# One gather tile in every eighth group of a graph-network kernel, fetched row by row from SyncE

## The chip, the cores and the metric

The kernel runs on one core of a Trainium2 chip. The metric is the device time of one launch, in microseconds, taken as the median of several runs.

The core has five engines that the text names: TensorE (PE for its matmuls, PEld for its weight loads), VectorE (DVE), ScalarE (ACT), GpSimd (POOL) and SyncE (SP), which computes nothing and issues DMAs. [...] A suffix q, as in SPq, is the engine's own sequencer, where DMA issues, register loads and waits stand.

## What is computed

One message-passing layer over a graph of 6250 nodes with 128 features and 100,000 edges that are sorted by destination. Cut to what matters:

```python
msg_in = concat([x[src], x[dst], edge_attr], axis=1)       # 100000 x 260
h = silu(msg_in @ mW1 + mb1)
messages = h @ mW2 + mb2
aggregated = segment_sum(messages, dst, num_segments=6250)
u = silu(concat([x, aggregated], axis=1) @ uW1 + ub1)
out = layernorm(x + layernorm(x + (u @ uW2 + ub2)))
```

Everything is float32. The first matrix is split by rows, so that the part of `x[src]` can be multiplied before the rows are gathered: a table `tab_a = x @ mW1[:128]` is made once in HBM, and an edge then needs one row of it, 512 bytes. This gather of 100,000 rows is what the change touches.

## The kernel before, in words

The edges are cut into groups of 1024, eight tiles of 128 edges each (`G = 8`, `GE = 1024`), which makes 98 groups, the last one shorter. One pass of the main loop (L688) handles one group. The order of instructions on every engine is the order in which the program writes them, as a manual schedule is in force for all five engines.

In pass g the following stand in this order:

- `load(g + 4)` (L593) on SP. It fetches `mv`, 96 rows of a second table `tab_b` that begin at a row number held in a register (L599), and `st`, the edge attributes (L600). Every fourth time it also fetches `near` (L320), the destination numbers of four groups at once, 384 KB; every 14th time `load_bases` (L344) loads 14 row numbers from SBUF into registers of SP and DVE. The `mv` buffers are five, so the fetch for group g + 4 has to wait until TensorE has done the products of group g - 1. In some passes other DMAs are issued by SP too: `xs` and `out_dram` of a node batch (L495, L572), and the turning of edge attributes (L306, L313).
- `hidden(g)` (L640): DVE adds the gathered rows `ga` and the products `pre` into `s` (L648), ACT makes `h` of it (L649).
- `products(g + 2)` (L627) on TensorE (L631), from `st` and `mv`.
- `node_matrix(g + 3)` (L602), which reads `near` (DVE, L604), and `edge_matrix(g + 1)` (DVE, L617).
- `by_nodes(g)` (L665), the segment sum of the group by matmuls (TensorE, L660), and its addition to the accumulator two passes later.
- `fetch(g + 2)` (L273): eight gathers on POOL, one for each tile (L277). Each reads 128 row numbers from SBUF[...] and starts their transfer into `rows[g + 2][:, i, :]`. The first of them waits for the first product of group g + 2, the fifth for the first sum of group g.
- a step of each node batch that is under way.

SP has eight semaphores for its DMAs and takes them in turn. Before it issues a DMA it therefore waits until the DMA eight places earlier has landed.

Of the kernel before, what the change touches and what calls it, by code (L numbers as in the profile page):

```python
# [8 lines left out]
F32 = mybir.dt.float32  # L9
I32 = mybir.dt.int32  # L10
# [4 lines left out]
ENG = mybir.EngineType  # L15
# [3 lines left out]
P = 128  # L19
EPS = 1e-5  # L20
IN_RANGE = "indices of nodes, which the reference takes to be in range"
# [3 lines left out]
def kernel(  # L25
# [40 lines left out]
    nc = tc.nc  # L66
    N, H = x.shape
# [4 lines left out]
    G = 8  # L72
    GE = G * P
    NG = -(-E // GE)
# [2 lines left out]
    NW = NP + W  # L77
    K1 = W + ED
    RB = 14
    CLOSE = 14  # L80
    LEAD = 4
    RAW = 5
# [7 lines left out]
    EJ = EC // EQ  # L90
    assert NG % RB == 0 and EC * NC == E and EJ * EQ == EC

# [16 lines left out]
    work = edges.enter_context(tc.tile_pool(name="edge", bufs=2))  # L109
# [154 lines left out]
    tab_a = dram.tile([NP, H], F32, name="tab_a")  # L264
# [2 lines left out]
    near_d = dram.tile([NG, GE], U8, name="near_d")  # L267
    rows, bases, near = {}, {}, {}

    def tiles_of(g):  # L270
        return min(G, -(-(E - g * GE) // P))

    def fetch(g, *after):  # L273

        rows[g] = gath.tile([P, G, H], F32, name="ga")
        for i in range(tiles_of(g)):
            ins = nc.gpsimd.indirect_dma_start(  # L277
                out=rows[g][:, i, :],
                out_offset=None,
                in_=x if g < RAW else tab_a[:, :],  # L280
                in_offset=bass.IndirectOffsetOnAxis(
                    ap=src_i[:, g, i : i + 1] if g else src_0[:, i : i + 1], axis=0
                ),
            )
            part, at = divmod(i * len(after), G)
            if after and at == 0 and after[part]:
                tc.add_manual_dep(
                    ins.ins,
                    after[part].ins.name,
                    mybir.DependencyInfo(  # L290
                        mybir.DependencyClass.Sync, mybir.DependencyReason.DATA
                    ),
                    reason="TensorE keeps up with the gathers",
                )

    fetch(0)


# [4 lines left out]
    def attributes(c):  # L303
        t = turn.tile([EQ, EJ * ED], F32, name="ea_l")
        chunk = edge_attr[c * EC : (c + 1) * EC]
        nc.sync.dma_start(t, chunk.rearrange("(q j) d -> q (j d)", q=EQ))  # L306
        ea_l[c] = t
# [7 lines left out]
    def destinations(g):  # L315

        n = min(NQ, NG - g)
        t = work.tile([W, NQ, GE], U8, name="near")
        flat = near_d[g : g + n].rearrange("(o g) e -> o (g e)", o=1)
        nc.sync.dma_start(  # L320
            t[:, :n].rearrange("w g e -> w (g e)"), flat.to_broadcast([W, n * GE])
        )
        for k in range(n):
            near[g + k] = t[:, k, :]
# [18 lines left out]
    def load_bases(g):  # L343
        _, vals = nc.values_load_multi_w_load_instructions(  # L344
            base_i[0:1, g : g + RB],
            engines=(ENG.SP, ENG.DVE),
            min_val=0,
            max_val=NP,
            skip_runtime_bounds_check_because=IN_RANGE,
        )  # L350
        for k, v in enumerate(vals):
            bases[g + k] = v
# [63 lines left out]
    ps = edges.enter_context(tc.tile_pool(name="edge_ps", bufs=2, space=PSUM))  # L416
# [5 lines left out]
    def node_y():  # L422
        return node_ps.tile([P, BT, H], F32, name="y")
# [13 lines left out]
    def load_weights():  # L437
        for name, shape in (("w2", [P, H]), ("u1a", [P, H]), ("mb2", [P, 1])):
            raw_w[name] = work.tile(shape, F32, name=f"raw_{name}", bufs=1)
        nc.sync.dma_start(raw_w["w2"], mW2)  # L440
        nc.sync.dma_start(raw_w["u1a"], uW1[P:])
        nc.sync.dma_start(raw_w["mb2"], mb2.rearrange("(f o) -> f o", o=1))
        nc.sync.dma_start(u1x, uW1[:P])
        nc.sync.dma_start(u2, uW2)
        nc.sync.dma_start(ub1_col, ub1.rearrange("(f o) -> f o", o=1))
        nc.sync.dma_start(ub2_row, ub2.rearrange("(o f) -> o f", o=1))
        for t, row in ((g_b, ln_g), (b_b, ln_b), (ub2_b, ub2)):
            nc.sync.dma_start(t, row.rearrange("(o f) -> o f", o=1).to_broadcast([P, H]))

    def fuse_weights():  # L450
        pm = node_y()
        nc.tensor.transpose(pm[:, 0, :], raw_w["w2"], ident)
        yield
        w2T = work.tile([P, P], F32, name="w2T", bufs=1)
        nc.scalar.copy(w2T, pm[:, 0, :])
        yield
        nc.tensor.matmul(pm[:, 1, :], w2T, raw_w["u1a"], start=True, stop=True)
        nc.tensor.matmul(pm[0:1, 2, :], raw_w["mb2"], raw_w["u1a"], start=True, stop=True)
        yield
        nc.scalar.copy(w2u, pm[:, 1, :])  # L460
        nc.vector.memset(mb2u, 0.0)
        for k in range(DQ):
            nc.scalar.copy(mb2u[32 * k : 32 * k + 1], pm[0:1, 2, :])
# [129 lines left out]
    def load(g):  # L593

        if g % NQ == 0 and g:
            destinations(g)
        if g % RB == 0 and g:
            load_bases(g)
        nc.sync.dma_start(mv[g % NM][:W], tab_b[bass.ds(bases[g], W), :])  # L599
        nc.sync.dma_start(stbuf[g % NST][W:], ea_d[:, g * GE : (g + 1) * GE])  # L600

    def node_matrix(g):  # L602

        nc.vector.tensor_scalar(  # L604
            stbuf[g % NST][:W],
            near.pop(g),
            p_next,
            0.0,
            op0=OP.is_equal,
            op1=OP.add,  # L610
            accum_out=deg_q[g // DQ % 2][:, g % DQ * 32 : g % DQ * 32 + 1],
        )
# [27 lines left out]
    def hidden(g):  # L640
        h = hbuf[g % NH]
        ga = rows.pop(g)
        n = tiles_of(g)
        s = pre.pop(g)
        if g >= RAW:
            ps = s
            s = work.tile([P, G, H], F32, name="s")
            nc.vector.tensor_add(s[:, :n], ga[:, :n], ps[:, :n])  # L648
        nc.scalar.activation(h[:, :n], s[:, :n], AF.Silu)  # L649
        return h  # L650

# [13 lines left out]
    def by_nodes(g, h, oh):  # L665

        pt = degrees(g)
        sums(g, pt, h, oh, 0, tiles_of(g))
        return pt
# [18 lines left out]
    for g in range(NG):  # L688
        if g == 1:
            load_weights()  # L690
        if g == 2:
            running.append(destination_checks(node_y()))
        if g == 8:
            running.append(fuse_weights())
        for c in range(1, NC):
            if g == max(1, c * EC // GE - 10):
                attributes(c)
            if g == max(1, c * EC // GE - 10) + 1:
                attribute_rows(c)
        if g + LEAD < NG:  # L700
            load(g + LEAD)
        last = g >= NG - 1
        if not last:
            h[g] = hidden(g)
        if g + 2 < NG:
            pre[g + 2] = products(g + 2)
        if g + MADE < NG:
            node_matrix(g + MADE)
        if g + 1 < NG:
            oh[g + 1] = edge_matrix(g + 1)  # L710
        if g - 2 in pt:
            add(g - 2, pt.pop(g - 2))
        if last:
            break
        pt[g] = by_nodes(g, h.pop(g), oh.pop(g))
        if CLOSE <= g + 2 < NG:
            fetch(g + 2, begun[g + 2], summing[g])
        elif g == 0:
            fetch(7, ended[1], begun[2])
        elif g == 1:  # L720
            fetch(8, begun[3], summing[1])
        elif g % 2:
            fetch(g // 2 + 8, ended[g + 1], begun[g + 2] if g == CLOSE - 3 else ended[g + 2])
        if g >= NG - 3:
            add(g - 1, pt.pop(g - 1))
        for i0, n, first in batches[:-1]:
            if g == (first if first >= NG - 3 else first + 1):
                running.append(node_batch(i0, n, *node_tiles(nodes, node_y)))
        for _ in range(0 if g == NG - 2 else 4 if g == NG - 3 else 2 if g >= NG - 6 else 1):
            advance(running)  # L730
        if g == NG - 3:
            final = node_batch(
                *batches[-1][:2],
                nodes,

                lambda name, p=P: gath.tile([P, G, H], F32, name="ga")[:p, :BT],
                lambda: rows_ps()[:, :BT],
                final=True,
            )
            next(final)  # L740
        if g == NG - 2:
            next(final)

    g = NG - 1
    n = tiles_of(g)
    ga, pg, oh_g, h_g = rows.pop(g), pre.pop(g), oh.pop(g), hbuf[g % NH]
    s = work.tile([P, G, H], F32, name="s")
# [27 lines left out]
    def all_nodes():  # L775
        with tc.tile_pool(name="nodes_g", bufs=2) as nodes:
            with tc.tile_pool(name="nodes_g_ps", bufs=1, space=PSUM) as node_ps:
                for i0, n, _ in batches:
                    y = lambda: node_ps.tile([P, BT, H], F32, name="y")
                    running = [node_batch(i0, n, *node_tiles(nodes, y))]  # L780
                    while running:
# [4 lines left out]
                         skip_runtime_bounds_check_because="the result of a comparison")  # L786
# [143 lines left out]
```

## Time and profile before

| | us |
|---|---|
| time before, median of 3 runs (1167.98 to 1169.18) | 1169.08 |
| time of the profiled execution | 1007.52 |
| its span, first to last instruction | 1005.4 |
| POOL busy | 740.0 (74%) |
| PE busy | 682.9 (68%) |
| DVE busy | 487.0 (48%) |
| ACT busy | 238.9 (24%) |
| mean granted TensorE clock | 0.739 |

The profiled execution is shorter than the timed runs by 161.56 us: the timed ones are 1.160 times as long. Durations below are those of the profiled execution. A group's line gives the summed busy time and the mean of one instruction, then the idle time of the engine ahead of it and what ended most of that. "Issue" is time in which the engine waited for nothing that the profile shows. Instructions of a sequencer, among them all DMA issues and register loads of SP, are not counted as busy.

### The profile page before, as it was taken

The page shows a single profiled execution, that of the slowest core. Times are in us where ns is not written, and L with a number is a line of the kernel's source. Part 1 is how long each engine was busy: PE and PEld are TensorE (multiplying, and loading weights), DVE is VectorE, ACT ScalarE, POOL GpSimd, SP SyncE. Part 2 cuts the span into 40 slices and gives each one's busy share as a digit, 9 for nine tenths or more (in the row PEclk, how much of TensorE's full clock was granted, in tenths as well). Part 3 has the DMA queues.
Part 4 walks back from the last instruction along what each step waited for, and adds up shares of the span by engine and source line. Part 5 has one row for each costly group of instructions (what it writes and reads, how often), then busy time and mean ns, then how long its engine had stood idle before and what let it go on. Part 6 is the DMA issues. An engine that isn't in the chain of part 4 may idle for free. (4 is left out here: it accounts for less than half of the span.)

```text
span 1005.4 us, 11309 instructions
## 1 busy us (share of the span) xinstructions
PE 682.9 (68%) x3645; PEld 627.6 (62%) x3645; DVE 487.0 (48%) x1018; ACT 238.9 (24%) x295; POOL 740.0 (74%) x790
## 2 busy tenths in 40 slices
PE   5869766577676567757676756767757666766854
PEld 4759756567666566756665755766656666565752
DVE  5667625444544543643554453544453454264455
ACT  2312212220321131231222122122023113122233
POOL 7767777777777777777777777777777777777771
PEclk9979977777767677667667667667767775867776
DMA  9954332232323322333233224232332332322221
GB/s 229 266 159 115 98 76 58 75 93 77 85 75 83 85 76 57 86 83 97 54 96 87 68 63 113 60 93 65 88 84 75 83 75 76 83 59 76 66 76 29
DMA packets 70076, 89.01 MB, mean 89 GB/s; under 512 B 20703, under 2 KB 51694, under 8 KB 70010
## 3 DMA queue, kind: packets, MB, share of 16 engines
q0 software_dynamic: 25024, 51.30, 20.7%
q1 hardware_dynamic: 40408, 35.03, 12.4%
q10 hardware_dynamic: 4578, 1.89, 0.9%
q8 instruction: 31, 0.51, 0.2%
q14 instruction: 35, 0.29, 0.1%
HBM read 76.78 MB, written 11.38 MB: 88 GB/s over the span
## 5 line engine op out<-in xcount | busy, mean ns | idle before, releaser
L277 POOL DMA_INDIRECT ga<-tab_a,src_i x742 | 700.7, 944 | 231.1 <-issue 210.0
L631 PE MATMUL pre<-mv,st 100*128 100x128 f32 x1564 | 328.6, 390 | 282.1 <-DVE s L648 235.6
L631 PEld LDWEIGHTS pre<-mv,st 100*128 100x128 f32 x1564 | 300.5, 293 | 304.4 <-DVE s L648 255.5
L648 DVE TENSOR_TENSOR s<-ga,pre 128x1024 f32<-128x1024 f32 x92 | 112.3, 1221 | 460.1 <-DMA ga<-tab_a,src_i 459.5
L660 PE MATMUL pt<-oh,h 128*128 128x96 f32 x1564 | 254.0, 332 | 7.2 <-DVE deg L678 3.9
L660 PEld LDWEIGHTS pt<-oh,h 128*128 128x128 f32 x1564 | 252.9, 253 | 9.4 <-ACT acc_b L500 3.3
L649 ACT ACTIVATE h<-s 128x1024 f32<-128x1024 f32 x92 | 97.2, 1057 | 649.1 <-DVE s L648 649.1
L604 DVE TENSOR_SCALAR_CACHE_REDUCE st<-near,p_next 96x1024 f32<-96x1024 uint8 x98 | 124.2, 1269 | 2.2 <-issue 1.4
L617 DVE TENSOR_TENSOR oh<-w_row,rel 128x768 f32<-128x768 f32 x98 | 93.0, 949 | 11.5 <-PE pt L660 11.5
L277 POOL DMA_INDIRECT ga<-in_x_dram,src_i x32 | 30.3, 948 | 9.8 <-issue 8.8
L649 ACT ACT_TABLE_LOAD x23 | 29.5, 1283 | 26.0 <-DMA raw_mb<-in_L_gnn_mb_dram 19.6
L489 ACT ACT_TABLE_LOAD x24 | 30.8, 1283 | 7.9 <-DVE mv L484 7.5
L530 PEld LDWEIGHTS y<-u,uT 128*128 128x128 f32 x94 | 22.5, 323 | 8.9 <-issue 8.9
L530 PE MATMUL y<-u,uT 128*128 128x128 f32 x94 | 25.2, 415 | 0.0
L678 DVE TENSOR_TENSOR deg<-deg,pt 1x96 f32 x98 | 24.4, 249 | 1.0
L673 DVE TENSOR_TENSOR acc<-acc,pt 128x96 f32 x98 | 23.6, 241 | 0.1
L377 PE MATMUL wide<-w,xT 128*128 128x256 f32 x98 | 23.1, 391 | 0.2 <-DVE rel L200 0.2
L377 PEld LDWEIGHTS wide<-w,xT 128*128 128x128 f32 x98 | 18.9, 198 | 2.9 <-DVE rel L200 0.4
L484 DVE BATCH_NORM_AGGREGATE mv<-st 128x2 f32<-128x6 f32 x98 | 17.8, 182 | 3.4
L568 ACT ACTIVATE z<-z,shift,r 128x128 f32<-128x128 f32 x47 | 19.2, 479 | 0.3 <-DVE shift L562 0.3
L545 DVE SCALAR_TENSOR_TENSOR z<-y,r,xs 128x128 f32<-128x128 f32 x47 | 16.5, 351 | 1.7
L542 DVE SCALAR_TENSOR_TENSOR y<-y,mv,g_b 128x128 f32<-128x128 f32 x47 | 16.5, 351 | 1.3
(118 smaller groups left out, 327.5 us busy)
## 6 DMA issues: line engine op xcount, KB each, us to landing
ga<-tab_a,src_i POOLq DMA_INDIRECT x742, 2.6
near<-near_d SPq DMA_DIRECT2D x24, 384.0 KB
mv<-tab_b SPq DMA_DIRECT2D x98, 48.0 KB
tab_a<-t SPq DMA_DIRECT2D x6, 512.0 KB
tab_b<-x_sb SPq DMA_DIRECT2D x6, 512.0 KB
xs<-in_x_dram SPq DMA_DIRECT2D x11, 256.0 KB
out_dram<-z SPq DMA_DIRECT2D x11, 256.0 KB
st<-ea_d SPq DMA_DIRECT2D x98, 16.0 KB
```

The costliest lines, as they stand in the source:

```text
L277: ins = nc.gpsimd.indirect_dma_start(out=rows[g][:, i, :], out_offset=None, in_=x if g < RAW else tab_a[:, :], in_offset=bass.IndirectOffs ...
L377: ins = nc.tensor.matmul(pm[:, j], xT[:, cols], w1, start=True, stop=True)
L489: nc.scalar.activation(r[:, :n], mv[:, :n, 1], AF.Sqrt, bias=eps)
L530: nc.tensor.matmul(y[:, i, :], by_p[:, :, i], u2, start=final, stop=final or i == n - 1)
L604: nc.vector.tensor_scalar(stbuf[g % NST][:W], near.pop(g), p_next, 0.0, op0=OP.is_equal, op1=OP.add, accum_out=deg_q[g // DQ % 2][:, g % D ...
L617: nc.vector.tensor_tensor(oh, w_row[:, None, :].to_broadcast([P, G, W]), rel[:, g, :, None].to_broadcast([P, G, W]), op=OP.is_equal,)
L631: ins = nc.tensor.matmul(pre[:, i, :], st[:, i, :], mv[g % NM], start=True, stop=g >= RAW)
L648: nc.vector.tensor_add(s[:, :n], ga[:, :n], ps[:, :n])
L649: nc.scalar.activation(h[:, :n], s[:, :n], AF.Silu)
L660: ins = nc.tensor.matmul(pt[:, :W], h[:, i, :], oh[:, i, :], start=i == 0, stop=i == tiles_of(g) - 1)
L673: nc.vector.tensor_add(at, at, pt[:, :W])
L678: nc.vector.tensor_add(at, at, pt[row, W:])
```

## The change

In nine groups, 24, 32, 40 and so on to 88, the eighth tile is no longer gathered by POOL. SP fetches it, one DMA of 512 bytes for each of its 128 rows, with the row number in a register. The work for such a tile is spread over eight passes: in each of the passes from `to - 10` to `to - 3`, after `load`, SP loads 16 row numbers into registers with one instruction and issues 16 DMAs. In the first of these passes it also fetches the 128 row numbers into SBUF. The tile has a buffer of its own, `ga_s`, so DVE adds it to the products in an instruction of its own, and the other addition is one tile shorter.

```diff
+    SPAN = 8
+    by_sync = {g: None for g in range(CLOSE + SPAN + 2, NG - SPAN + 1, SPAN)}
     def fetch(g, *after):
         rows[g] = gath.tile([P, G, H], F32, name="ga")
-        for i in range(tiles_of(g)):
+        for i in range(tiles_of(g) - (g in by_sync)):
             ins = nc.gpsimd.indirect_dma_start(
...
+    def fetch_by_sync(g):
+        for to in by_sync:
+            k = g - (to - SPAN - 2)
+            if not 0 <= k < SPAN:
+                continue
+            lo, hi = k * P // SPAN, (k + 1) * P // SPAN
+            if k == 0:
+                by_sync[to] = work.tile([P, H], F32, name="ga_s")
+                sources = work.tile([1, P], I32, name="src_s")
+                e0 = (to * G + G - 1) * P
+                nc.sync.dma_start(sources, src[e0 : e0 + P].rearrange("(o p) -> o p", o=1))
+                source_rows[to] = sources
+            _, vals = nc.values_load_multi_w_load_instructions(
+                source_rows[to][0:1, lo:hi],
+                engines=(ENG.SP,),
+                min_val=0,
+                max_val=N - 1,
+                skip_runtime_bounds_check_because=IN_RANGE,
+            )
+            for p, v in zip(range(lo, hi), vals):
+                nc.sync.dma_start(by_sync[to][p : p + 1, :], tab_a[bass.ds(v, 1), :])
...
     def hidden(g):
...
             s = work.tile([P, G, H], F32, name="s")
+            if g in by_sync:
+                n -= 1
+                nc.vector.tensor_add(s[:, n], by_sync[g], ps[:, n])
             nc.vector.tensor_add(s[:, :n], ga[:, :n], ps[:, :n])
+            n = tiles_of(g)
         nc.scalar.activation(h[:, :n], s[:, :n], AF.Silu)
...
         if g + LEAD < NG:
             load(g + LEAD)
+        fetch_by_sync(g)
```

In the built program SP has, for each row, a register operation that works out the address and the DMA; the row's DMA waits for nothing but its semaphore's turn. POOL's list is shorter by nine gathers and otherwise the same. DVE has nine additions of 128x128 more, each of which waits for all eight DMA semaphores of SP.

More of the change, by code (lines that the diff above doesn't have):

```diff
@@ L600, in load @@
         nc.sync.dma_start(stbuf[g % NST][W:], ea_d[:, g * GE : (g + 1) * GE])
+    def fetch_by_sync(g):
[19 more added lines that the diff above has]
+                nc.sync.dma_start(by_sync[to][p : p + 1, :], tab_a[bass.ds(v, 1), :])
+    source_rows = {}
     def node_matrix(g):
```

## The prediction, made before the changed kernel ran

> **What bounds the kernel now.** I began with the busy table and the costliest groups. No engine is over 74% busy, but POOL's gathers have idle time ahead of them that nothing ended:
>
> ```profile
> L277 POOL DMA_INDIRECT ga<-tab_a,src_i x742 | 700.7, 944 | 231.1 <-issue 210.0
> L648 DVE TENSOR_TENSOR s<-ga,pre 128x1024 f32<-128x1024 f32 x92 | 112.3, 1221 | 460.1 <-DMA ga<-tab_a,src_i 459.5
> ...
> SPq L599 <- PE pre L631: 274.9, 39, 10.8
> SPq L572 <- ACT z L568: 166.4, 11, 21.2
> SPq L313 <- ACT ea_t L311: 158.3, 9, 27.4
> SPq L495 <- DVE st L483: 129.4, 11, 32.8
> ```
>
> POOL's 0.94 us and the 0.30 us after it are one step. The timeline of POOL shows them back to back:
>
> ```profile
> 499.52 0.94 POOL L277 DMA_INDIRECT ga<-tab_a,src_i  x1 [0.31 <-issue]
> 500.77 0.94 POOL L277 DMA_INDIRECT ga<-tab_a,src_i  x1 [0.30 <-issue]
> 502.01 0.94 POOL L277 DMA_INDIRECT ga<-tab_a,src_i  x1 [0.30 <-issue]
> ```
>
> So a gather costs 1.249 us, 782 of them 977 us of the 1005.4, and eight make the pass of 9.99 us (s starts 159.9 us into the span in pass 14 and 879.3 in pass 86). DVE waits for gathers in nearly every pass. SP, last four lines of the first fence (time waited, times, longest), sleeps most of the time. What it does when it is awake matters here, so I read its own timeline and the durations of its instructions:
>
> ```profile
> 68.10 0.30 SPq L446 DMA_DIRECT2D ub_row<-in_L_gnn_ub_dram  x1
> ...
> 503.65 0.33 SPq L599 DMA_DIRECT2D mv<-tab_b  x1
> 504.02 0.33 SPq L600 DMA_DIRECT2D st<-ea_d  x1
> 504.58 0.33 SPq L599 DMA_DIRECT2D mv<-tab_b  x1
> ...
> L344 SPq TENSOR_LOAD <-base_i x7: 1356/3068/3358, 46.6 to 795.4; - x7
> ...
> L599 SPq FUSED_REGOPS  x98: 37/37/51, 58.9 to 933.5; - x98
> L599 SPq MOVE mv<-tab_b x98: 29/29/37, 59.1 to 933.6; - x98
> ```
>
> One `mv` and one `st` that wait for nothing take 504.58 - 503.65 = 0.93 us. A load of 14 registers takes 1.36 or about 3.1 us (minimum, median and maximum are shown).
>
> [...] Here the issue time is the whole matter, as the trace shows the DMA engines 0.31 busy from 150 to 880 us. [...] The trace agrees in the long loads (3068 / 14 = 219 ns) and not in the short ones (1356 / 14 = 97 ns). [...] the timed runs are 1.160 times the profiled one, in a kernel whose span is 97% gather steps. I take the gap between them for a scale, not for a constant, and multiply by 1.16.
>
> **Part by part.** *Removed:* nine gathers on POOL, 9 x 1.249 = 11.2 us, while POOL sets the pace. *DVE:* nine additions of 128x128, near 0.25 us each (the 128x96 addition at L673 means 241 ns), nine others shorter by an eighth (0.15 us), and some 0.3 us of semaphore waits: under 0.5 us in nine passes, hidden under DVE's waits for gathers (394 us from 150 to 880). Without that cover it is 4 us. *DMA traffic:* 1152 rows less on one queue, as many more on another: nothing.
>
> *SP, per pass, in passes 14 to 85:* the row's step is FUSED_REGOPS to MOVE 0.09, MOVE to DMA 0.06, the DMA, and 0.04 to the next. Single-row DMAs took 0.22 to 0.27 us (four lists at L131 and L133, 2.6 and 4 KB) and 0.30 us (`ub_row`, 512 bytes). I take 0.28, which makes 0.475; the ends are 0.42 and 0.52 (with the 0.33 of `mv`). Sixteen are 7.6 us. The register load of 16: at 97 ns 1.55 us, at 219 ns 3.5. Of the loads before, those whose first byte lies on a multiple of 16 were short, but for the first, which ran at 46.6 us, when the DMA engines were at 99%; the others were long. The new loads all begin on a multiple of 16, so I take 1.59 with the gap behind it. With `mv` and `st` 0.94, `near` every fourth pass 0.09, the node and attribute DMAs 0.17, the fetch of row numbers with its landing (0.37 + 2.2 in eight passes, as a load must wait for it) 0.32, the register load of L344 0.16 and occasional slow issues (1.64 and 1.68 us in the trace) 0.13, a pass costs SP **11.0 us**. Before, the same sum without the change was 1.5.
>
> That is more than the 9.99 us of POOL's pass. SP becomes the bound, but not at once. It runs ahead: in pass 20 it had issued its loads at 216.4, s began at 222.8, so the lead was 6.4 us (in undisturbed passes about 24, but the waits at L495, L572 and L313 bring it back to the engines every eight to ten passes). And it can fall behind a little, because loads are for later groups. The tightest is `near`: pass 4m - 4 of SP issues what DVE needs in pass 4m - 3, landing after some 4.6 us; with the addition after it, s of pass 4m - 2 starts 8 us after SP's pass began, two passes (22.6 us) earlier in number, so the engines may be 14.6 us ahead of SP. `mv` is needed in pass g + 2 and the rows in pass `to`, three passes after the last are issued: looser. From pass 20 to 86, 66 passes: 66 x (11.0 - 9.99) = 67 us late, less 6.4 and 14.6, leaves 46 us. Behind the late `near` stands DVE's own queue (L604, then L617 and the next s), and TensorE and ACT wait for those. POOL can fill up to 7 us of its lead meanwhile, which it gives back in the tail after pass 86, where SP is free: +39 us. The 11.2 us taken from POOL are worth nothing once SP is the bound. 1007.5 + 39 = 1046.5 for the profiled execution. Times 1.16 it is 1214[...]. I forecast **1222 us**.
>
> **The rivals.**
> - *The register load is long.* 3.5 instead of 1.55: a pass costs 12.95, 66 x 2.96 = 195, less 21 and 7, +167; times 1.16 it is 1169 + 194 = 1363. For it: [...] four of seven loads of SP before. Against it: the three short ones, and the alignment.
> - *The rows land late.* A row waits for the DMA eight places ahead of it. Eight steps are 3.8 us; `st`, 16 KB, landed in 2.4 us at the median, `near` in 4.6 (from issue to the last update of its semaphore). If rows behind others took 4.6, the step is 0.575, the pass 12.6, and the time +144 x 1.16, 1336. Against it: 512 bytes each.
> - *SP keeps up.* If a row costs 0.42 and all else stands, the pass is 10.1 and the lead and lag of 21 us cover 66 passes of 0.1. From 0.42 us a row and below, the nine gathers are saved whole: 11.2 x 1.16 = 13, 1156 us, faster. For it: the four list DMAs of 0.22 to 0.27; against it: `ub_row`, the one with the rows' size.
> - *Nothing to measure:* a pass of about 10.4, where saving and delay cancel, 1169.
>
> **How the numbers follow.** The forecast, 1190 to 1265, has 0.50; the long load 0.27; late landings 0.10; SP keeping up 0.09; no change 0.04. The sums of the first three and of the last two give slower 0.87, faster 0.09, same 0.04, where a measurement of this kernel can tell about 0.2% (2.3 us) from no change. The range leaves out SP keeping up and the far end of long loads (above 1385): 1168 to 1385.
>
> **What would show it.** In the profile of the changed kernel: nine gathers fewer, and POOL idle ahead of others than "issue"; SP's waits for PE and DVE nearly gone from pass 25 on; DVE waiting for `near` at L604, or PE for `mv`; passes of about 11 us in the middle, and of 10 at the end; TENSOR_LOAD of `src_s` at 1.4 to 1.6 us; rows 0.475 us apart. Rows under 0.43 apart, or DVE still waiting for gathers in every pass, would prove me wrong; so would loads of 3.5 us.

## The result, and the profile after

| | us |
|---|---|
| before, median of 4 runs (1167.98 to 1172.19) | 1169.13 |
| after, median of 4 runs (1359.54 to 1369.36) | 1365.1 |
| ratio, with its 95% interval | 1.1656 [1.1637, 1.1676] |
| after, profiled execution | 1369.36 |
| its span | 1367.6 |

The change made the kernel 16.6% slower. DVE's part of `node_matrix`, which reads `near`, had hardly waited before:

```profile
L604 DVE TENSOR_SCALAR_CACHE_REDUCE st<-near,p_next 96x1024 f32<-96x1024 uint8 x98 | 124.2, 1269 | 2.2 <-issue 1.4
```

These are the groups of the changed kernel (POOL's gathers, DVE's part of `node_matrix`, the addition):

```profile
L280 POOL DMA_INDIRECT ga<-tab_a,src_i x733 | 692.4, 945 | 586.8 <-issue 205.6
L632 DVE TENSOR_SCALAR_CACHE_REDUCE st<-near,p_next 96x1024 f32<-96x1024 uint8 x98 | 124.4, 1270 | 404.1 <-DMA near<-near_d 401.9
L679 DVE TENSOR_TENSOR s<-ga,pre 128x1024 f32<-128x1024 f32 x92 | 110.9, 1205 | 264.3 <-DMA ga<-tab_a,src_i 229.7
```

There are nine gathers fewer, and one still takes 0.945 us. But POOL, which had idled 231.1 us ahead of them, now idles 586.8 us ahead of them, and only 205.6 of that is the 0.30 us between two gathers. DVE, which waited 459.5 us for gathers, now waits 229.7 us for them and 401.9 us for `near`, a transfer of SP. The waits of the changed kernel (us in total, times, longest) show how far this reaches:

```profile
DVE st L632 <- DMA near<-near_d: 401.9, 18, 27.8
...
PE pre L659 <- DMA st<-ea_d: 236.6, 23, 15.3
...
POOL ga L280 <- PE pt L692: 142.1, 18, 11.4
```

And SP's own waits, in the same columns:

```profile
SPq L575 <- ACT z L571: 56.2, 3, 30.2
SPq L498 <- DVE st L486: 37.0, 1, 37.0
...
SPq L316 <- ACT ea_t L314: 24.4, 2, 19.7
SPq L626 <- DMA ga_s<-tab_a: 14.8, 27, 1.4
...
SPq L602 <- PE pre L659: 9.0, 3, 4.5
```

TensorE waits for `st`, another of SP's transfers, and POOL waits for TensorE. SP hardly waits for the engines any more: the four waits that came to 729.0 us before come to 126.6 now (56.2, 37.0, 24.4 and 9.0), and from 330 to 1240 us into the span all waits of SP together are 15.2 us. So SP is the bound. From pass 20 to pass 86 the additions `s` start 14.56 us apart ((1221.6 - 260.4) / 66).

What SP does in a pass stands in its timeline, DMAs of one line drawn together:

```profile
608.32 0.70 SPq L603 DMA_DIRECT2D st<-ea_d  x1
611.90 11.52 SPq L626 DMA_DIRECT2D ga_s<-tab_a  x16
```

Sixteen rows took 11.52 us here (11.44 in the mean of these passes, 6.58 to 21.0), 0.72 for one. Yet the durations of SP's instructions (minimum, median, maximum in ns) give a cheap row in the median:

```profile
L618 SPq TENSOR_LOAD <-src_s x72: 38/1212/1393, 174.3 to 1227.6; - x72
...
L626 SPq FUSED_REGOPS  x1152: 2/37/1395, 175.5 to 1240.5; - x192
L626 SPq MOVE ga_s<-tab_a x1152: 2/29/1389, 175.6 to 1240.5; - x192
L626 SPq DMA_DIRECT2D ga_s<-tab_a x1152: 2/228/1385, 175.6 to 1240.6; - x192
```

A MOVE of 29 ns in the median takes up to 1389, and a register operation up to 1395. None of these 2304 instructions is a DMA, and in the trace none of them names a semaphore. Read one by one, the instructions of the pass above start in parts at 0.08 us intervals (in the first profile the MOVE of `mv` at L599 starts 0.078 to 0.084 us after its register operation in the four cases with nothing between them), and in parts at 611.90, 612.61, 613.33: 0.70 us apart, whatever they are. I call that a hold. The minima are as odd as the maxima: 2 ns for a DMA that takes 228 in the median, so inside such a stretch a recorded duration is not what the instruction costs; the starts are what I go by. Where holds stand, and that not every run has them, came out of the experiments. What makes them did not.

### The profile page after: what moved, and what is told of

The parts are those of the page before. It is cut to its first block, busy times and chain, and to the rows that moved or that the text cites. A ratio compares the mean times of both kernels' runs of the same rounds, so it can differ in the third digit from the quotient of the medians.

```text
span 1367.6 us, 14885 instructions
## 1 busy us (share of the span) xinstructions
PE 708.0 (52%) x3645; PEld 636.4 (47%) x3645; DVE 488.2 (36%) x1027; ACT 238.0 (17%) x295; POOL 731.8 (54%) x781
## 5 line engine op out<-in xcount | busy, mean ns | idle before, releaser
L280 POOL DMA_INDIRECT ga<-tab_a,src_i x733 | 692.4, 945 | 586.8 <-issue 205.6
L659 PE MATMUL pre<-mv,st 100*128 100x128 f32 x1564 | 308.3, 368 | 337.7 <-DMA st<-ea_d 236.6
L659 PEld LDWEIGHTS pre<-mv,st 100*128 100x128 f32 x1564 | 284.9, 276 | 357.5 <-issue 336.3
L692 PE MATMUL pt<-oh,h 128*128 128x96 f32 x1564 | 280.6, 344 | 254.4 <-DVE acc L705 157.1
L692 PEld LDWEIGHTS pt<-oh,h 128*128 128x128 f32 x1564 | 266.1, 259 | 267.9 <-issue 219.9
L632 DVE TENSOR_SCALAR_CACHE_REDUCE st<-near,p_next 96x1024 f32<-96x1024 uint8 x98 | 124.4, 1270 | 404.1 <-DMA near<-near_d 401.9
L679 DVE TENSOR_TENSOR s<-ga,pre 128x1024 f32<-128x1024 f32 x92 | 110.9, 1205 | 264.3 <-DMA ga<-tab_a,src_i 229.7
L314 ACT COPY ea_t<-ea_l 80x500 f32<-80x500 f32 x10 | 10.8, 1082 | 183.9 <-DMA ea_l<-in_edge_attr_dram 183.9
L280 POOL DMA_INDIRECT ga<-in_x_dram,src_i x32 | 30.7, 959 | 16.6 <-issue 8.5
L380 PE MATMUL wide<-w,xT 128*128 128x256 f32 x98 | 27.2, 437 | 7.7 <-DVE x_sb L383 7.7
L524 PE MATMUL y<-ub_row,ones 1*128 1x512 f32 (+1 forms) x24 | 21.7, 994 | 11.9 <-ACT uT L521 11.7
L710 DVE TENSOR_TENSOR deg<-deg,pt 1x96 f32 x98 | 24.4, 249 | 1.0
L521 ACT ACTIVATE uT<-y,ub_col 128x512 f32<-128x512 f32 (+1 forms) x12 | 8.1, 675 | 80.3 <-remote 62.9
```

What stands on the lines that cost most here:

```text
L280: ins = nc.gpsimd.indirect_dma_start(out=rows[g][:, i, :], out_offset=None, in_=x if g < RAW else tab_a[:, :], in_offset=bass.IndirectOffs ...
L380: ins = nc.tensor.matmul(pm[:, j], xT[:, cols], w1, start=True, stop=True)
L632: nc.vector.tensor_scalar(stbuf[g % NST][:W], near.pop(g), p_next, 0.0, op0=OP.is_equal, op1=OP.add, accum_out=deg_q[g // DQ % 2][:, g % D ...
L659: ins = nc.tensor.matmul(pre[:, i, :], st[:, i, :], mv[g % NM], start=True, stop=g >= RAW)
L692: ins = nc.tensor.matmul(pt[:, :W], h[:, i, :], oh[:, i, :], start=i == 0, stop=i == tiles_of(g) - 1)
L710: nc.vector.tensor_add(at, at, pt[row, W:])
```

## The experiments

Two theories stood after the result. Theory 1: the chip of the timed runs executes everything some 1.16 times as slowly (the prediction's scale), and SP's rows are dear. Theory 2: the engines are as fast as in the first profile, and something stalls single instructions of SP and TensorE.

The runs came in four groups, each on a chip of its own, each with the kernel before run beside it. Which chips the first profile and the result came from is not on record. The table counts gaps of 0.67 to 0.74 us between the starts of neighbouring instructions of SP, and of neighbouring weight loads of TensorE (PEld), in the traces; it was made once all groups had run, and it is the key to the rest.

| group, before beside it (us) | kernel | SP | PEld |
|---|---|---|---|
| the first profile of before (1007.52) | before | 2 | 1 |
| that of the result (1169.13) | after | 401 | 38 |
| e1 (1163.17) | before | 29 | 46 |
| e1 | e1_static | 298 | 45 |
| e2 (1008.32) | e2_both | 1 | 1 |
| e3 (1008.11) | e3_after | 2 | 1 |
| e4 (1163.63) | e4_after | 414 | 35 |
| e4 | e4_half | 398 | 36 |
| e4 | e4_double | 345 | 28 |

Weight loads alone give too small a number for TensorE. With matmuls and weight loads in one order there are 167 such gaps in e1_before and 1 in the first profile. Where the kernel before takes 1163 to 1169 us there are holds; where it takes 1008 there are next to none. By its time, the first profile of before belongs to the second kind, and all its timed runs to the first. I speak of chips with and without holds. But every chip was used in one group only, so the runs do not tell a property of the chip from a state that it was in at the time.

**e1_before: the kernel before again.** Not edited.

> The kernel before itself, for a profile beside its timed runs. Theory 1 (a scale: everything on the chip of the timed runs takes 1.16 times as long): 1169 us, with POOL's gather step near 1.45 us instead of 1.249. Theory 2 (the engines run as in the first profile, but something stalls one of them): 1169 us with a gather step of 1.25 us in most places and about 160 us of stalls elsewhere.

1162.81 us beside 1163.17, 0.9998 [0.9989, 1.0007]. POOL's timeline of this run:

```profile
608.48 0.95 POOL L277 DMA_INDIRECT ga<-tab_a,src_i  x1 [0.31 <-issue]
609.73 0.94 POOL L277 DMA_INDIRECT ga<-tab_a,src_i  x1 [0.30 <-issue]
613.14 0.95 POOL L277 DMA_INDIRECT ga<-tab_a,src_i  x1 [2.47 <-remote]
614.39 0.95 POOL L277 DMA_INDIRECT ga<-tab_a,src_i  x1 [0.30 <-issue]
```

The step of a gather is 609.73 - 608.48 = 1.25 us, as in the first profile (median 1.252, and 1.249 there). What is new is the gap of 2.47 us ahead of the gather at 613.14, put down to an event that the trace didn't keep:

```profile
POOL ga L277 <- remote: 144.0, 49, 3.4
```

The gathers themselves tell what was awaited. Of the 55 gathers of `tab_a` with more than 0.45 us of idle time ahead of them, 54 wait for TensorE's semaphore, with 155.1 us of idle time in all; in the first profile there is one, with 1.5. TensorE's timeline of the same stretch shows why it was late:

```profile
608.55 0.32 PE L660 MATMUL pt<-oh,h 128*128 128x96 f32 x1 [0.88 <-issue]
609.95 0.32 PE L660 MATMUL pt<-oh,h 128*128 128x96 f32 x1 [1.08 <-issue]
611.35 0.32 PE L660 MATMUL pt<-oh,h 128*128 128x96 f32 x1 [1.08 <-issue]
612.07 0.52 PE L660 MATMUL pt<-oh,h 128*128 128x96 f32 x1 [0.40 <-issue]
612.78 0.54 PE L660 MATMUL pt<-oh,h 128*128 128x96 f32 x2 [0.19 <-issue]
```

Sums of by_nodes that follow each other within 0.3 us elsewhere start 1.40 and 0.70 us apart here (a weight load stands between two of them), with nothing that they wait for. The fifth gather of a pass waits for the first sum, the first for the first product, so POOL pays. The pass is 11.51 us ((1016.1 - 256.7) / 66), against 9.95 in the first profile. Theory 1 falls: DVE's addition takes 1220 ns in the mean beside 1221, ACT's activation 1056 beside 1057. Only TensorE's granted clock is lower, 0.685 beside 0.739, but its matmuls are 2 to 3% longer (398 ns beside 390 at L631, 341 beside 332 at L660), not 16%. Theory 2 is what the trace shows.

**e1_block: the rows as one DMA of 16 rows per pass, from fixed addresses, without register loads.** In this kernel, and in e1_static and the double ones, the rows fetched for the nine tiles aren't the sources' but the table's first 128.

```diff
...
-            for p, v in zip(range(lo, hi), vals):
-                nc.sync.dma_start(by_sync[to][p : p + 1, :], tab_a[bass.ds(v, 1), :])
+            nc.sync.dma_start(by_sync[to][lo:hi, :], tab_a[lo:hi, :])
```

> The nine tiles are fetched by SP as one DMA of 16 consecutive rows in each pass, from fixed addresses, with no register loads; so the gathered rows of the nine tiles are not those of the sources. It leaves POOL's saving and takes SP's work away. Theory 1 (POOL sets the pace when SP has little to do): 11 to 13 us under the kernel before, about 1157. Rival (DVE's extra addition and its wait for SP's semaphores cost as much as the nine gathers): 1169 or more.

1150.34 us, 0.9897 [0.9877, 0.9918], pass 11.34. The nine gathers are worth 12.8 us on a chip with holds when SP's part is next to nothing, as the first theory expected; the additions on DVE don't eat the gain.

**e1_static: sixteen DMAs of one row, fixed addresses, no register work.**

```diff
...
-            for p, v in zip(range(lo, hi), vals):
-                nc.sync.dma_start(by_sync[to][p : p + 1, :], tab_a[bass.ds(v, 1), :])
+            for p in range(lo, hi):
+                nc.sync.dma_start(by_sync[to][p : p + 1, :], tab_a[p : p + 1, :])
```

> The 16 DMAs of one row in each pass stay, but from fixed addresses, without register loads and address operations: one instruction for a row instead of three. The fetched rows are not those of the sources. Theory 1 (SP's time is the sum of its instructions): 16 x 0.33 + 1.5 = 6.8 us a pass, under POOL's, so about 1157. Theory 2 (the 0.70 us stalls on SP come with the issue of many DMAs in a row): still far above before, 1300 or more. Theory 3 (the stalls come with the number of instructions, whatever they are): one third of the instructions, so most of the loss is gone, 1160 to 1220.

1160.28 us, 0.9977 [0.9963, 0.9991]. Rows stand 0.295 us apart in the median, so 16 would be 4.7 us; they took 7.28 in the mean. The sixteen DMAs alone don't make the kernel slower, so theory 2 of this run (1300 or more) falls, though holds come into these DMAs too. Of the 12.8 us that e1_block gained, 2.9 are left; which wait takes the rest isn't settled. The time fits the lower end of theory 3; e4 puts that theory to a harder test.

**e1_loads: only the row numbers and the register loads, gathers as before.**

```diff
...
-            for p, v in zip(range(lo, hi), vals):
-                nc.sync.dma_start(by_sync[to][p : p + 1, :], tab_a[bass.ds(v, 1), :])
...
```

> Only the fetch of the 128 row numbers and the load of 16 registers in each pass stay on SP; no row DMAs, and POOL gathers all eight tiles as before. All theories: about the time before, 1169 to 1173, as SP has 5 us to spare in each pass; above 1190 the register loads themselves hold SP up.

1163.56 us, 1.0003 [0.999, 1.0015]. The run says nothing of register loads: as nothing used the registers, the built program had none of the loads left, and only the nine fetches of 512 bytes remained. It was a mistake in the experiment, and no other run has the register loads without the rows.

**e2_both: the change, and POOL gathers all eight tiles as well** (the eighth is not used in the nine groups).

```diff
-        for i in range(tiles_of(g) - (g in by_sync)):
+        for i in range(tiles_of(g)):
...
```

> The changed kernel with POOL's nine gathers put back: SP fetches the rows and DVE uses them, and POOL gathers all eight tiles too, of which the eighth is not used in the nine groups. Theory 1 (SP's pass is the bound, POOL's saving is worth nothing): the same time as the changed kernel, 1360 to 1368. Rival (POOL's pace still enters): some 11 to 13 us more, 1375.

1007.61 us beside 1008.32, 0.9992 [0.9983, 1.0001]. Every number expected here was near 1365, and none came, as this chip has no holds; the question that the run asked stays without an answer where there are holds. It still tells something: with POOL's work put back and SP's 1152 rows kept, nothing is lost. Here SP's rows are free.

**e2_half: eight rows per pass, over sixteen passes (four tiles in all).**

```diff
-    SPAN = 8
+    SPAN = 16
```

> SPAN = 16: every 16th group instead of every eighth, so four tiles, eight rows in each pass, in registers as in the change. Theory 1 (a row costs SP 0.715 us with its stalls, whatever the number): 8 x 0.715 + 1.2 + 1.9 = 8.8 us a pass, under the 11.5 of the other engines, so no bound: between the saving of four gathers (1158) and the small loss that e1_static showed beside e1_block (1168). Rival (any row DMA in a pass delays mv, st and near enough to cost in proportion): half of the loss, about 1260.

1003.11 us, 0.9946 [0.993, 0.9963]: 5.2 us gained, where four gathers are 5.0. The expectation was for a chip with holds; e4_half meets it.

**e2_shared: eight rows on SP, eight on ACT's queue, per pass.**

```diff
+            mid = (lo + hi) // 2
+            for eng, of, a, b in ((nc.sync, ENG.SP, lo, mid), (nc.scalar, ENG.Activation, mid, hi)):
...
+                for p, v in zip(range(a, b), vals):
+                    eng.dma_start(by_sync[to][p : p + 1, :], tab_a[bass.ds(v, 1), :])
```

> The change with its rows divided: SP and ACT each load eight registers and issue eight rows in each pass; ACT's stand ahead of its activation of the same pass, where it waits for DVE. Theory 1 (the issue time of one sequencer is what costs): SP 8.8 and ACT 5.7 + 1.0 + 2.4 = 9.1 us a pass, both under 11.5, so near e1_static, 1150 to 1175. Rival (ACT's activation comes late behind its row DMAs, or both sequencers wait for each other's turns of the eight semaphores): 1200 or more.

997.45 us, 0.9887 [0.9871, 0.9904]: 10.9 us gained, nearly the whole of the nine gathers (11.2). This expectation too was for a chip with holds.

**e2_double: 32 DMAs per pass, each row in two halves of 256 bytes, fixed addresses.**

```diff
...
+            for p in range(lo, hi):
+                for c in (0, H // 2):
+                    cols = slice(c, c + H // 2)
+                    nc.sync.dma_start(by_sync[to][p : p + 1, cols], tab_a[p : p + 1, cols])
```

> As e1_static, but each row in two DMAs of 256 bytes: 32 DMAs of one instruction each in a pass, from fixed addresses (other rows than the sources'). Measured so far: 16 rows took SP 11.44 us at the mean in the changed kernel (6.58 without any stall) and 7.28 in e1_static (4.7 without). Theory 1 (a stall comes with instructions and DMAs alike, 0.46 us a DMA in all): 32 x 0.46 + 1.9 = 16.5 us a pass, about 1490 us. Theory 2 (the stalls come with the number of instructions alone, 0.10 us each): 32 x 0.295 + 3.3 + 1.9 = 14.6 a pass, about 1365. Theory 3 (with the number of DMAs alone, 0.30 each): 21 a pass, 1750 or more.

1073.35 us, 1.064 [1.0619, 1.0662]. This is the prediction's mechanism without holds. SP's timeline of this run:

```profile
604.03 0.32 SPq L603 DMA_DIRECT2D st<-ea_d  x1
604.39 9.38 SPq L617 DMA_DIRECT2D ga_s<-tab_a  x32
614.33 0.34 SPq L602 DMA_DIRECT2D mv<-tab_b  x1
614.73 0.31 SPq L603 DMA_DIRECT2D st<-ea_d  x1
615.09 9.52 SPq L617 DMA_DIRECT2D ga_s<-tab_a  x32
```

32 DMAs take 9.4 us. The pass in the fence costs SP 10.70 (from `st` to `st`), and with `near` and the DMAs of node batches the fetches of `mv` stand 11.32 us apart from pass 20 to 86, 1.33 more than POOL's 9.99. In pass 20 SP issues its loads 4.7 us ahead of `s`, in pass 86 17.4 behind: an allowance of 22.1 us, where the prediction had 6.4 and 14.6. Its arithmetic up to there gives 66 x 1.33 - 21 = 67 us. Measured: 1073.35 - 1008.32 = 65.0. The 7 us that the prediction then took off, for gathers that POOL would do ahead of time, would make it 60. DVE waits for `near`, as foreseen:

```profile
DVE st L623 <- DMA near<-near_d: 179.6, 15, 16.3
```

**e3: the change once more, and three of these, on another chip.** The edits are those above.

> The changed kernel again, as the runs so far came from two chips: on one the kernel before takes 1163 us and its trace has instructions of SP and PE that take 0.70 us each in bursts, on the other it takes 1008 us without them. Theory 1 (what slows the change is these stalls, which make a row's step 0.715 us instead of 0.41): beside a before of 1008 the change is faster by the whole saving of POOL, 996 to 999, as a pass costs SP 9.6 us; beside a before of 1163 it is 1355 to 1370. Theory 2 (the loss belongs to the change wherever it runs): 1.16 times the kernel before on any chip.

> Eight rows a pass, four tiles. Theory 1: beside a before of 1008, 1003 as measured; beside a before of 1163, 8.8 us a pass, no bound but SP's stalls, 1158 to 1175.

> Eight rows a pass on SP and eight on ACT. Theory 1: beside a before of 1008, 997 as measured; beside a before of 1163 each sequencer has about 9 us of work in a pass of 11.5, so 1150 to 1180. Rival (stalls on ACT delay its activations, which stand in the chain from s to the sums): 1200 or more.

> 32 DMAs of 256 bytes in a pass, from fixed addresses, again. Beside a before of 1008 theory 1 expects 1073 as measured (a pass of 11.3 us); beside a before of 1163, where 16 such DMAs took 7.28 us, 16.5 us a pass and 1450 to 1500.

| | us (before 1008.11) | ratio |
|---|---|---|
| e3_after | 997.31 | 0.9895 [0.9879, 0.9912] |
| e3_half | 1004.09 | 0.9958 [0.9942, 0.9975] |
| e3_shared | 997.27 | 0.9892 [0.9875, 0.9909] |
| e3_double | 1074.02 | 1.0655 [1.0634, 1.0676] |

The very kernel that was 16.6% slower in the result is 1.05% faster on this chip. SP's timeline of e3_after shows a whole pass and the start of the next:

```profile
600.91 0.32 SPq L602 DMA_DIRECT2D mv<-tab_b  x1
601.28 0.34 SPq L603 DMA_DIRECT2D st<-ea_d  x1
603.08 6.45 SPq L626 DMA_DIRECT2D ga_s<-tab_a  x16
609.59 0.32 SPq L323 DMA_DIRECT2D near<-near_d  x1
610.15 0.32 SPq L602 DMA_DIRECT2D mv<-tab_b  x1
...
619.83 0.33 SPq L602 DMA_DIRECT2D mv<-tab_b  x1
```

From `mv` to `mv` SP needs 610.15 - 600.91 = 9.24 us in this pass and 9.68 in the next, which has a DMA of a node batch in it. That is less than POOL's 9.99. The durations of SP's instructions in e3_after tell why:

```profile
L618 SPq TENSOR_LOAD <-src_s x72: 1136/1221/1637, 136.7 to 856.3; - x72
...
L626 SPq FUSED_REGOPS  x1152: 37/37/42, 137.9 to 863.8; - x192
L626 SPq MOVE ga_s<-tab_a x1152: 29/29/29, 138.0 to 863.9; - x192
L626 SPq DMA_DIRECT2D ga_s<-tab_a x1152: 224/228/280, 138.1 to 863.9; - x192
```

The medians are those of the kernel after the change, but the maxima are 42, 29 and 280 ns instead of 1.39 us. Sixteen rows take 6.73 us in the mean and 7.45 at most; one step is 0.412. The waits of e3_after show the same bound as before the change:

```profile
DVE s L679 <- DMA ga<-tab_a,src_i: 402.3, 80, 8.7
POOL ga L280 <- issue: 221.9, 728, 0.3
```

DVE waits for gathers again, and in 728 of its gaps POOL has nothing ahead of it but its own 0.30 us. The margin is small, though: in passes 20 to 86 SP issues its loads only 1.0 to 7.1 us before the `s` of the same pass begins, where before the change it was 6.1 to 27.0. And sharing with ACT gains nothing over the change here (997.27 us beside 997.31), as there is nothing to relieve.

**e4: the same four on one more chip, which turned out to have holds.** The edits are those above.

> The changed kernel. Beside a before of about 1163: 1355 to 1370, with 0.70 us instructions on SP in its trace; beside a before of about 1008: 996 to 999, without them.

> Eight rows a pass. Beside a before of 1163: SP's pass is 8.8 us, under the 11.5 of the other engines, 1158 to 1175. Beside a before of 1008: 1003 to 1005.

> Eight rows a pass on SP and eight on ACT. Beside a before of 1163: 1150 to 1180 if one sequencer's time is what costs; 1200 or more if stalls of ACT delay its activations. Beside a before of 1008: 997.

> 32 DMAs of 256 bytes a pass from fixed addresses. Beside a before of 1163: if stalls come with instructions and DMAs alike, 16.5 us a pass and 1450 to 1500; with the number of instructions alone 14.6 and about 1365; with the number of DMAs alone 21 and over 1700. Beside a before of 1008: 1073 again.

| | us (before 1163.63) | ratio | rows per pass: mean us, and the same in e3 |
|---|---|---|---|
| e4_after | 1343.1 | 1.1534 [1.1488, 1.1581] | 11.15, 6.73 |
| e4_half | 1167.12 | 1.0025 [1.0002, 1.0047] | 8.52, 3.37 |
| e4_shared | 1197.33 | 1.0283 [1.019, 1.0375] | |
| e4_double | 1306.04 | 1.1216 [1.1169, 1.1263] | 12.11, 9.84 |

The slowdown comes again where there are holds (pass 14.27), if a little smaller than expected (1355 to 1370). The half one came as expected, and nowhere near half of the loss (1260, the rival of e2_half). The double kernel, far the worst of the four without holds, came out *faster* than the change, below everything expected of it. Holds add 4.4 us to the change's 48 instructions of rows per pass (16 each of register operation, MOVE and DMA), 5.2 to the 24 of half, 2.3 to the 32 of double, which are DMAs alone, and in e1_static 2.6 to 16 DMAs (7.28 beside the 4.7 worked out from its step). So it is neither so much for an instruction nor so much for a DMA; register-addressed rows suffer some 5 us a pass, rows with fixed addresses some 2.5. Which rule makes these sums stays open.

The shared kernel's two runs give 1.9 to 3.8% more than before, between its two expectations. ACT has 73 gaps of 0.7 us there, where it had one in e3_shared, and its own rows now hold it up, as the rival had it: its timeline has seven of them drawn over 11.90 us.

```profile
608.00 1.28 ACT L683 ACT_TABLE_LOAD   x1 [10.67 <-issue]
609.29 1.06 ACT L683 ACTIVATE h<-s 128x1024 f32<-128x1024 f32 x1
...
613.22 11.90 ACTq L628 DMA_DIRECT2D ga_s<-tab_a  x7
```

No version that fetches the right rows beats the kernel before both with and without holds. The half one comes nearest: 0.4 to 0.5% faster without holds, 0.25% slower with them (0.02 to 0.47).

## Why the prediction was wrong

The kernel got slower, as forecast, but that was luck. The prediction's own sum for a chip like that of the first profile was 1046.5 us, 39 us slower than 1007.5; on such a chip the change took 997.31 (e3_after), 10.8 us faster than before. Where the kernel did get slower, it was by 196 us instead of 53, and through holds, which the prediction didn't know of. The chain from a late SP to the other engines was right. Step by step:

- *POOL sets the pace, a pass is 9.99 us, nine gathers are worth 11.2.* Right where there are no holds: the change gained 10.8 us (1008.11 - 997.31). With holds POOL waits for TensorE as well, and the nine were still worth 12.8 (e1_block).
- *"a pass costs SP **11.0 us**".* **This step failed, for both kinds of chip.** Without holds it is 9.65, under POOL's 9.99, so SP isn't the bound at all. The row's step is 0.412, not 0.475: the DMA is 0.228, so the four list DMAs of 0.22 to 0.27 were the right row to read and `ub_row`, with its equal size, was not. The register load is 1.21, not 1.55. These make 16 x 0.063 + 0.34 = 1.35 us less, 9.65, and SP's timeline in e3_after shows 9.24 and 9.68. With holds the pass measured 14.56: they put 11.44 - 6.73 = 4.7 us on the rows of a pass, and 9.65 + 4.7 = 14.4. The rest of SP's instructions have holds too.
- *"I take the gap between them for a scale, not for a constant, and multiply by 1.16."* **This step failed as well.** It was my estimate from two times, 1169.08 and 1007.52 us, and no run here shows such a scale: the gather step is 1.249 to 1.252 us in every trace. The 8 us by which the forecast of 1222 exceeds 1214 rested on no trace either. The gap goes with holds on TensorE and SP. A common scale leaves the order of SP's pass and POOL's as it is; holds change it, as they lengthen SP's rows (6.73 us a pass without them, 11.44 with them) and not POOL's step.
- *The nine additions on DVE, and the DMA traffic, cost nothing.* Nothing contradicts it: in e2_both, which keeps them and POOL's work, the time doesn't move (1007.61 us beside 1008.32).
- *Lead and lag of 21 us, `near` the tightest, DVE, TensorE and ACT behind it.* Right: e2_double used up 22.1. (The 14.6 in it rests on 22.6 us for two passes, where two of 11.0 are 22.0.) In the changed kernel with holds SP was already 25.9 us behind `s` in pass 20, so the allowance was used up by then: passes 20 to 86 alone lost 66 x (14.56 - 11.51) = 201 us, beside 196 for the whole kernel. The 11.51 is e1_before's.
- *The rivals.* "SP keeps up", given 0.09, is what happens without holds, by its own condition (0.42 us a row and below). The long register load came nearest in time, 1363, for a reason that did not occur: 16 registers took 1.21 us in the median, 76 ns a register, where the long loads of the kernel before had shown 219 (3068 ns for 14). The rows didn't land late either: 27 waits of SP for its rows, 14.8 us in all.
- *The signs.* POOL idling for others, SP's waits nearly gone and DVE waiting for `near` all came. "Rows under 0.43 apart" came too, the sign of being wrong: their median was 0.416 with holds and 0.412 without.
- *What would have told.* The profile of before was of a chip without holds, and its time, 1007.52, didn't belong to the runs of 1169. That gap was 161 us, larger than anything the change could save. I saw it and gave it a cause that no line showed.

## What to carry to other kernels

When a profiled execution and the timed runs differ by far more than their scatter, the profile may be, as here, of a chip that behaves otherwise: don't scale it, say that the cause is unknown and widen the range for a cost that falls on one engine alone. Work moved to a sequencer needs a margin, not just a fit: here 9.65 us in a pass of 9.99 gained 1% without holds and lost 15 to 17% with them, while half as many rows gained 0.4 to 0.5% and lost 0.25%. And a queue that feeds everybody (`mv`, `st`, `near`) is the wrong place for fine-grained work, because its lateness reaches the others: in the changed kernel with holds DVE waited 401.9 us for `near`, TensorE 236.6 for `st`, and POOL 142.1 and 112.1 for TensorE.

## What the runs showed of the hardware

- Holds: in the traces of the result, of e1 and of e4, SP's and TensorE's instructions, and ACT's once it issued rows (73 such gaps in e4_shared), start 0.70 us apart, register operations as well as DMAs; SP's 401 gaps in the trace of the result stand one to nine in a row. In the first profile, e2 and e3 there are next to none (1 or 2 on SP in the traces of the table). The step of the gathers on POOL was 1.249 to 1.252 us on both. The kernel before takes 1163 us with them and 1008 without; in e1_before's trace the idle time of POOL behind TensorE's semaphore, 155.1 us, is about as long as that difference.
- The traces with holds also keep fewer records of DMAs landing: 3350 in e1_before and 6231 in the trace of the result, against 16283 in the first profile of before. In these three the two went together. With the holds went a lower granted TensorE clock: 0.66 to 0.70 in the runs with holds, 0.71 to 0.75 in those without. Whether keeping records makes the holds, or both have another cause, was not tried: a span and a granted clock are on record for every run, so no run here seems to have been free of tracing.
- DMAs of one row with the address in a register stood 0.412 us apart on SP (512 bytes in e3_after), those with a fixed address 0.295 (512 bytes in e1_static) and 0.294 (256 bytes in e2_double). A load of 16 registers took 1.22 us (e3_after), one of eight 0.77 (e2_half).
